# Attention stage of a two-layer image kernel: phases of two slots over seven PSUM banks, waits bank by bank, sums in an idle bank

## The chip, the core and the metric

The kernel runs on one core of a Trainium2 chip. The metric is device time in microseconds (us) of one launch. The engines of the core that matter here are TensorE (PE in the profile, with its weight loads as PEld), ScalarE (ACT), VectorE (DVE), GpSimd (POOL) and the DMA queue of SyncE (SP). Each engine takes its instructions in the order written and waits on semaphores for the others. SBUF is the large on-chip memory; PSUM is the small one that TensorE writes, eight banks of 128 partitions by 512 float32.

## The reference

Two layers run on `x` of shape (2, 256, 64, 64), so two images of 256 channels and 4096 positions. Layer 0 is a state-space block and isn't touched. Layer 1 is attention with eight heads of 32 channels, without an output projection:

```python
x = x + _L0_conv_ref(_gn(x), ...)
x = x + _L1_conv_ref(_gn(x), L1_conv_qkv_w, L1_conv_qkv_b, 8)

# _L1_conv_ref: n = 4096, head_dim = 32
qkv = jnp.einsum('bchw,oc->bohw', x, qkv_w) + qkv_b[None, :, None, None]
qkv = qkv.reshape(b, 3, num_heads, head_dim, n)
q, k, v = (qkv[:, 0], qkv[:, 1], qkv[:, 2])
attn_logits = jnp.einsum('bhci,bhcj->bhij', q, k) * scale
attn_weights = jax.nn.softmax(attn_logits, axis=-1)
out = jnp.einsum('bhij,bhcj->bhci', attn_weights, v)
```

`_gn` normalises groups of eight channels.

## The kernel before, in words

`mamba_stage` (layer 0) takes the first 2010 us or so and also prepares queries, keys and values of image 0. Then `attention` (line 969) works through image 0, prepares image 1 (`prepare`, line 1076) and works through image 1. It is written under a manual schedule: the order in the source is the order on every engine.

**Tiles and slots.** An image has two groups of four heads, and a group has 8 tiles of T = 512 queries, so 16 tiles per image, 32 in all. A tile goes over the 4096 keys in NC = 32 chunks of 128; one tile with one chunk is a *slot* (1024 slots in all), and `c` is the chunk's number. In a slot TensorE makes four matmuls of logits, one per head, keys on the partitions (`logits`, line 1151; matmul at L1162). ScalarE takes their exponentials from PSUM to SBUF (`exponentials`, L1175). TensorE then multiplies values by exponentials into `po`, four column groups of 32 at once (`values`, L1199).

**Row sums.** The denominators are sums of the exponentials over all 4096 keys. Over the partitions they are added by a matmul with `ones` at a tile's end; over the chunks, each head's part is added by another engine:

- Heads 0 and 1 go into `chunk`, a buffer with four places per element (a ring of two). When three new chunks are in it, DVE adds all four places into place 0 of the *other* buffer of the ring (`sum_chunk`, L1184), which the next three chunks fill up. This happens at c = 3, 6, 9, ... 30. At c = 30 the sum goes to `acc_sb` instead, and the exponentials of c = 31 go to a buffer of the ring `e`.
- Heads 2 and 3 go into a ring `e` of five buffers of 128x1024. POOL adds them into `acc_p`: both heads at once for 16 of the chunks (L1230, L1239), and head 3 alone (L1237) for the 15 chunks in `SHARED`, c in {8, 10, 12, 13, 14, 16, 18, 20, 21, 22, 24, 26, 28, 29, 30}. For those, DVE adds head 2 into `acc_2` (L1236; a copy, L1234, for the first). `acc_2` lies in a PSUM bank.

**The end of a tile.** `finish` (line 1241) is a generator that `Slots` resumes once per slot, between other work. It copies `po`, adds the parts (L1249, L1250), lets TensorE sum over the partitions into the PSUM bank of `acc_2` (L1257), copies the sums (L1260), takes reciprocals in four pieces (L1264), multiplies on POOL (L1267), adds bias and the residual (L1270), stores, and keeps two maxima for a range check (L1273, L1274). `end` does this for the last tile of all.

**Phases and PSUM.** Work goes in *phases*. A half slot (two heads) is a unit; a phase has three units, except that each tile ends with two phases of two. The eight banks are three pairs for logits (one tile of two banks per unit), one for `acc_2` and the sums, one for `po`. In step k of `run` (line 1314) ScalarE takes the exponentials of phase k, TensorE does the values of phase k-1 and then the logits of phase k+1. A unit's logits wait until ScalarE has read the pair three units earlier.

**What the code of the page shows as lines.** L1162 logits, L1199 values, L1175 exponentials, L1184 sums of `chunk`, L1236 adds into `acc_2`, L1237 and L1239 adds on POOL, L1250 and L1270 adds in `finish`, L1036 the normalisation of image 1, L463 a step of the group norm of layer 0.

Of the kernel before, what the change touches and what calls it, by code (L numbers as in the profile page):

```python
# [29 lines left out]
def group_norm_scales(nc, small, psum_tile, stats, gmat, eps_t, out):  # L30
# [9 lines left out]
    yield  # L40
    ps = psum_tile()
    for k in range(KC):
        nc.tensor.matmul(ps[:, k : k + 1], lhsT=gmat, rhs=mv[k][:, 0:1], start=True, stop=True)
    for k in range(KC):
        nc.vector.tensor_copy(out[k][:, 0:1], ps[:, k : k + 1])
# [7 lines left out]
    ps = psum_tile()  # L53
    for k in range(KC):
        nc.tensor.matmul(ps[:, k : k + 1], lhsT=gmat, rhs=e[k][:, 1:2], start=True, stop=True)
    yield
    for k in range(KC):
        nc.scalar.activation(e[k][:, 0:1], ps[:, k : k + 1], AF.Ln, bias=eps_t)
        nc.scalar.activation(out[k][:, 1:2], e[k][:, 0:1], AF.Exp, scale=-0.5)


class Slots:
# [10 lines left out]
    def run(self):  # L73
        for entry in list(self.waiting):
            if entry[0] <= self.now:
                try:
                    entry[0] = self.now + (next(entry[1]) or 1)
                except StopIteration:
                    self.waiting.remove(entry)
        self.now += 1  # L80

# [887 lines left out]
def attention(ctx, tc, stats, consts, w, outs, scratch, range_t):  # L969
# [18 lines left out]
    ps_s = ctx.enter_context(tc.tile_pool(name="l1pss", bufs=3, space=PSUM))  # L988
    ps_2 = ctx.enter_context(tc.tile_pool(name="l1ps2", bufs=1, space=PSUM))
# [10 lines left out]
    ep = ctx.enter_context(tc.tile_pool(name="l1e", bufs=5))  # L1000
# [8 lines left out]
    def s_tile():  # L1009
        return ps_s.tile([P, 2, T], F32, name="s", tag="s")  # L1010
# [11 lines left out]
    def load_x(t):  # L1022
        if t >= NT:
            return
        if t < 2:

            if t == 0:
                xn["q"] = p2.tile([P, 4, T], F32R, name="q").bitcast(F32)
            xn[t] = xn["q"][:, KC * t : KC * t + KC, :]
        else:  # L1030
            xn[t] = ep.tile([P, KC, T], F32, name="e")
# [8 lines left out]
    def project(t, i):  # L1040


        pm = s_tile()
        for m in range(KC):
            for c in range(KC):
                nc.tensor.matmul(  # L1046
# [5 lines left out]
                )  # L1052
        halves = chunk().rearrange("p q h t k -> p q (h t k)").rearrange("p q (m t) -> p q m t", t=T)
        for m in range(KC):
            bias = b_qkv[:, i * KC + m : i * KC + m + 1]
            nc.scalar.activation(halves[:, 0, m, :].bitcast(F32R), pm[:, m, :], AF.Identity, bias=bias)
            nc.vector.scalar_tensor_tensor(
                halves[:, 1, m, :].bitcast(F32R), pm[:, m, :], bias, halves[:, 0, m, :], ALU.add, ALU.subtract
            )
            nc.sync.dma_start(scratch.qk[KG + m, i, t].rearrange("s c h t -> (c h) s t"), halves[:, :, m, :])  # L1060

    def project_values(t):
        pm = s_tile()
        flat = pm.rearrange("p a t -> p (a t)")
        for j in range(T // P):
            for c in range(KC):
                nc.tensor.matmul(
# [6 lines left out]
        nc.scalar.copy(v[:, bass.ts(t, T // P), :].rearrange("p s c -> p (s c)"), flat)  # L1074
# [24 lines left out]
    def image(b):  # L1099
# [44 lines left out]
        sizes = [3] * ((2 * NC - 4) // 3) + [2, 2]  # L1144
        bounds = [0, *itertools.accumulate(sizes * (KG * NT))]
        PHASES = [range(*ends) for ends in zip(bounds, bounds[1:])]
        SHARED = [c for c in range(8, NC) if c % 8 in (0, 2, 4, 5, 6)]
        todo = {}
        tiles = {}

        def logits(s, half):
            if s >= S:
                return
            i, c = divmod(s, NC)
            kt, kj = divmod(c * P, T)
            if half == 0:
                todo[s] = Slot()
                todo[s].s, todo[s].e = [], []
            ps = s_tile()
            for j in range(2):  # L1160
                h = 2 * half + j
                nc.tensor.matmul(  # L1162
                    ps[:, j, :], lhsT=keys[i // NT, kt][:, h, kj : kj + P], rhs=queries[i][:, h, :], start=True, stop=True
                )
            todo[s].s.append(ps)

        def exponentials(s, half):
            if half == 0 and s % NC < NC - 1:
                k = place(s % NC)
                first = s % NC == 0 or k == 1 and s % NC > 1  # L1170
                todo[s].chunk = (todo.pop("chunk", None) or chunk()) if first else todo[s - 1].chunk
                e = todo[s].chunk[:, k // 2, :, :, k % 2]
            else:
                e = ep.tile([P, 2, T], F32, name="e")
            nc.scalar.activation(e, todo[s].s[half], AF.Exp, scale=SCALE)  # L1175
            todo[s].e.append(e)
# [9 lines left out]
        def values(first, end):  # L1186

            u = first
            while u < end:
                s, half = divmod(u, 2)  # L1190
                i, c = divmod(s, NC)
                g = i // NT
                width = 2 if half == 0 and u + 1 < end else 1
                cols = slice(half * T // 2, (half + width) * T // 2)
                u += width
                if c == 0 and half == 0:
                    tiles[i].po = ps_o.tile([P, T], F32, name="po")
                for h in range(4):
                    nc.tensor.matmul(  # L1199
                        tiles[i].po[h * D : (h + 1) * D, cols],  # L1200
                        lhsT=v[:, c, g * P + h * D : g * P + (h + 1) * D],
                        rhs=todo[s].e[h // 2][:, h % 2, cols],
# [7 lines left out]
        def add_up(s):  # L1210
            i, c = divmod(s, NC)
            tile_ = tiles[i]
            eb = todo[s].e[1]
            if last(i) and c == NC - 1:
                return
            if last(i) and c == NC - 2:
                pass
            elif c == NC - 2:
                tile_.acc = p1.tile([P, 3, T], F32, name="acc_sb")
                sum_chunk(s, tile_.acc[:, 0:2].rearrange("p h t -> p (h t)"))  # L1220
            elif place(c) == 3:
                todo["chunk"] = chunk()
                sum_chunk(s, todo["chunk"].rearrange("p q h t k -> p q (h t) k")[:, 0, :, 0])
# [7 lines left out]
            elif c in SHARED:  # L1231
                if c == SHARED[0]:
                    tile_.acc_2 = ps_2.tile([P, T], F32, name="acc_2", tag="a2")
# [7 lines left out]
        def finish(i):  # L1241
# [4 lines left out]
            po = p1.tile([P, T], F32, name="po_sb")  # L1246
            nc.vector.tensor_copy(po, d.po)
            acc = d.acc
            nc.vector.tensor_add(acc[:, 2, :], d.acc_2, d.acc_p[:, 0, :])  # L1249
            nc.vector.tensor_add(acc[:, 0:2, :], acc[:, 0:2, :], todo[i * NC + NC - 1].e[0])  # L1250
            res = p3.tile([P, T], F32, name="res")
            nc.sync.dma_start(res, x[g * P : (g + 1) * P, cols])
            yield 3
            ps = ps_2.tile([P, T], F32, name="sums_ps", tag="a2")
            for h in range(4):
                part = acc[:, h, :] if h < 3 else d.acc_p[:, 1, :]
                nc.tensor.matmul(ps[h * D : (h + 1) * D, :], lhsT=ones, rhs=part, start=True, stop=True)  # L1257
            yield
            sums = p1.tile([P, T], F32, name="sums")
            nc.vector.tensor_copy(sums, ps)  # L1260
            yield
            r = p1.tile([P, T], F32, name="r")
# [9 lines left out]
            at = b * KG * NT + i  # L1272
            nc.vector.tensor_reduce(range_t[:, 0, at : at + 1], sums, AX.X, ALU.max)  # L1273
            nc.vector.tensor_reduce(range_t[:, 1, at : at + 1], r, AX.X, ALU.max)  # L1274

        def end():
# [6 lines left out]
            ps = s_tile()[:, 0, :]  # L1283
            acc = p1.tile([P, T], F32, name="acc_end")
            nc.vector.tensor_copy(acc, d.acc_2)
            nc.scalar.activation(res, res, AF.Identity, bias=b_qkv[:, 2 * KC + g : 2 * KC + g + 1])
            terms = [[todo[S - 2].chunk[:, k // 2, h, :, k % 2] for k in range(4)] for h in range(2)]
            terms += [[d.acc_p[:, 0, :], acc], [d.acc_p[:, 1, :]]]

            def sum_up(rounds):  # L1290
                for n in rounds:
                    for h in range(4):
                        n_ = n - 4 + len(terms[h])
                        if 0 <= n_:
                            part = terms[h][n_] if n_ < len(terms[h]) else todo[S - 1].e[h // 2][:, h % 2, :]
                            nc.tensor.matmul(
                                ps[h * D : (h + 1) * D, :], lhsT=ones, rhs=part, start=(n_ == 0), stop=(n == 4)
                            )

            sum_up(range(4))  # L1300
            yield
            sum_up([4])
            r = p1.tile([P, T], F32, name="r")
            for j in range(T // P):
                nc.vector.reciprocal(r[:, bass.ts(j, P)], ps[:, bass.ts(j, P)])
# [5 lines left out]
            nc.vector.tensor_reduce(range_t[:, 0, at : at + 1], ps, AX.X, ALU.max)  # L1311
            nc.vector.tensor_reduce(range_t[:, 1, at : at + 1], r, AX.X, ALU.max)

        def run():
            k = 0
            while k <= len(PHASES) or b == 1 and side.waiting:
                for p in PHASES[k] if k < len(PHASES) else ():
                    s, half = divmod(p, 2)
                    i, c = divmod(s, NC)
                    if half == 0:  # L1320
                        if c == 0:
                            tiles[i] = Slot()
                            load_queries(i + 1)
                        if i % NT == NT - 1 and i < KG * NT - 1 and c % (T // P) == 0:

                            load_keys(i // NT + 1, c * P // T)
                        if b == 1 and 1 <= i <= KG:
                            nc.sync.dma_start(scratch.v[b * KG + i - 1, :, c, :], v[:, c, (i - 1) * P : i * P])
                        if b == 0 and s == S - 24:
                            load_x(0)  # L1330
                            load_x(1)
                        if b == 0 and s == S - 14:
                            normalise(0)
                    if k > 0 or b == 0:
# [225 lines left out]
```

## Time and profile before

| what | us |
|---|---|
| three runs, median (lowest, highest) | 4288.56 (4288.10, 4290.58) |
| the profiled execution: its time, its span | 4289.86, 4288.1 |
| layer 0, with the lead into attention | 0 to 2010 |
| image 0, 16 tiles | 2010 to 3085 |
| preparing image 1 | 3085 to 3180 |
| image 1, 16 tiles | 3180 to 4288 |

The share of busy time over the whole span (PE 96%, DVE 90%, ACT 87%, POOL 87%) is a mean of two unlike layers. In image 0 alone, a stretch of 1075 us, PE is busy 1069.7 us, ACT 1005.8, DVE 964.3 and POOL 940.7, so all four are within 13% of each other. The granted TensorE clock is 1.00 of full speed there, and the DMA engines are busy 16% of the time.

A row of a group reads: line, engine, operation, output <- inputs, shapes, count, then the sum of busy time in us, the mean of one in ns, and the idle time of the engine just before with what ended it. In a timeline the first number is the start, the second the duration, both in us; a number in brackets is the time that the engine stood idle before. Instructions of one engine can overlap at their ends, so the time from one start to the next is shorter than the duration.

### The profile page before, as it was taken

The numbers are of one execution on the slowest core, as the hardware profiler recorded it, in microseconds if no ns is written. First come the engines' busy times: TensorE is split into PE (matmuls) and PEld (weight loads), VectorE is DVE, ScalarE is ACT, GpSimd is POOL, SyncE is SP. The second block draws the span as 40 slices with busy tenths as digits, with TensorE's granted clock in tenths as the row PEclk, the third lists the DMA queues.
The fourth block names the chain that finished last, engine by engine and source line by source line (L and its number), as shares of the span: only waits on it lengthen the run. The fifth ranks groups of instructions, "written<-read, shape, count | busy, mean of one in ns | idle before, by whom it ended". The sixth has DMA issues, their size and how long they took to land.

```text
span 4288.1 us, 58982 instructions
## 1 busy us (share of the span) xinstructions
PE 4119.0 (96%) x21176; PEld 1802.7 (42%) x21176; DVE 3855.6 (90%) x3304; ACT 3729.2 (87%) x4983; POOL 3751.9 (87%) x1913
## 2 busy tenths in 40 slices
PE   6799999999999999988999999999999999999998
PEld 2233333333333343333444444444454444444443
DVE  6899999999999999994988989899849889898998
ACT  5789898999788888874999999999859999999997
POOL 3999999999899999994888988889728989888897
PEclk8899999999999999999999999999999999999999
DMA  6334333344444444447101040110181110401100
GB/s 212 105 114 130 113 113 126 129 133 133 150 144 163 154 141 142 142 167 168 34 24 28 18 106 18 28 30 21 40 262 46 40 28 18 106 18 28 30 21 9
DMA packets 172302, 389.58 MB, mean 91 GB/s; under 512 B 23392, under 2 KB 49760, under 8 KB 163808
## 3 DMA queue, kind: packets, MB, share of 16 engines
q1 hardware_dynamic: 171120, 383.37, 29.4%
q8 instruction: 168, 2.75, 0.3%
q10 hardware_dynamic: 880, 2.36, 0.3%
q14 instruction: 134, 1.10, 0.1%
HBM read 292.33 MB, written 93.32 MB: 90 GB/s over the span
## 4 chain that ended last, share of the span: by engine, by line
PE 82%; DVE 10%; ACT 3%; issue 2%; DMA 1%; POOL 1%; SPq 0%; DVEq 0%; POOLq 0%; ACTq 0%
PE s L1162 25%; PE po L1199 24%; PE mm L448 16%; DVE h L869 6%; PE y L901 4%; PE mm L688 4%; PE bn L448 2%; PE mm L647 2%; DVE bn L860 1%; PE s L1046 1%; PE y L899 1%; PE mm L684 1%; PE sums_ps L1257 1%; ACT da L853 1%; ACT L248 1%
## 5 line engine op out<-in xcount | busy, mean ns | idle before, releaser
L1184 DVE TENSOR_REDUCE chunk<-chunk 128x1024 f32<-128x4096 f32 x288 | 1269.9, 4409 | 169.5 <-ACT chunk L1175 168.2
L1239 POOL TENSOR_TENSOR acc_p<-acc_p,e 128x1024 f32<-128x1024 f32 x479 | 1165.1, 2432 | 121.2 <-ACT e L1175 96.6
L875 POOL TENSOR_TENSOR h<-h,c 128x1024 f32<-128x1024 f32 x512 | 1204.5, 2378 | 33.1 <-issue 15.7
L1162 PE MATMUL s<-q,k 128*128 128x512 f32 x4096 | 1155.0, 415 | 7.3 <-ACT chunk L1175 3.1
L1175 ACT ACTIVATE e<-s 128x1024 f32<-128x1024 f32 x1056 | 1081.8, 1028 | 91.4 <-PE s L1162 58.9
L1175 ACT ACTIVATE chunk<-s 128x1024 f32<-128x1024 f32 x992 | 1117.3, 1126 | 49.3 <-PE s L1162 22.5
L1199 PE MATMUL po<-chunk,v 128*32 128x512 f32 (+1 forms) x5248 | 1057.0, 521 | 0.0
L1199 PE MATMUL po<-e,v 128*32 128x512 f32 (+1 forms) x5504 | 1020.5, 500 | 4.2 <-ACT e L1175 4.2
L1162 PEld LDWEIGHTS s<-q,k 128*128 128x128 f32 x4096 | 713.9, 188 | 624.7 <-ACT e L1175 233.9
L853 ACT ACTIVATE da<-dt_rep,neg_a 128x512 f32<-128x512 f32 x1024 | 695.6, 702 | 107.9 <-DVE h L869 103.7
L1237 POOL TENSOR_TENSOR acc_p<-acc_p,e 128x512 f32<-128x512 f32 x480 | 622.3, 1297 | 95.5 <-ACT e L1175 65.7
L869 DVE TENSOR_TENSOR_SCAN h<-da,state,dbu 128x512 f32<-128x512 f32 x512 | 650.1, 1272 | 14.6 <-PE y L901 7.4
L869 DVE TENSOR_TENSOR_SCAN h<-da,state,bn 128x512 f32<-128x512 f32 x512 | 645.6, 1261 | 11.1 <-PE y L901 5.0
L864 POOL TENSOR_TENSOR dbu<-dtu_rep,b 128x1024 f32<-128x1024 f32 x176 | 418.0, 2375 | 18.8 <-issue 9.1
L448 PE MATMUL bn<-proj,pick 112*128 112x512 f32 x512 | 341.9, 669 | 89.1 <-DVE h L869 86.2
L248 ACT ACT_TABLE_LOAD x312 | 400.3, 1283 | 6.2 <-PEq L1550 0.7
L1199 PEld LDWEIGHTS po<-e,v 128*32 128x32 f32 x5504 | 251.6, 109 | 272.1 <-issue 105.3
L860 DVE TENSOR_TENSOR bn<-dtu_rep,bn 128x512 f32<-128x512 f32 x512 | 345.4, 677 | 18.0 <-PE bn L448 8.0
L1199 PEld LDWEIGHTS po<-chunk,v 128*32 128x32 f32 x5248 | 240.2, 108 | 251.2 <-issue 251.2
L1236 DVE TENSOR_TENSOR acc<-acc,e 128x512 f32<-128x512 f32 x448 | 309.5, 691 | 17.4 <-DVE acc L1236 0.5
L901 PE MATMUL y<-h,sum 128*32 128x512 f32 x2048 | 299.3, 613 | 6.9 <-POOL h L875 6.8
L448 PE MATMUL mm<-yn,w_in 128*128 128x512 f32 x512 | 255.2, 623 | 7.9 <-ACT yn L538 3.8
(163 smaller groups left out, 4182.9 us busy)
## 6 DMA issues: line engine op xcount, KB each, us to landing
dt_rep<-dt_dram SPq DMA_DIRECT2D x128, 512.0 KB, 5.0
dtu_rep<-dtu_dram SPq DMA_DIRECT2D x128, 512.0 KB, 5.3
k<-qk_dram SPq DMA_DIRECT2D x62, 512.0 KB, 7.6
q<-qk_dram SPq DMA_DIRECT2D x124, 256.0 KB, 4.8
b<-bc_dram SPq DMA_DIRECT2D x64, 256.0 KB, 3.1
c<-bc_dram SPq DMA_DIRECT2D x64, 256.0 KB, 3.8
dt_dram<-dt SPq DMA_DIRECT2D x64, 256.0 KB, 2.3
dtu_dram<-lw SPq DMA_DIRECT2D x64, 256.0 KB, 3.6
```

Source lines behind the costliest of these rows:

```text
L248: self.nc.scalar.preload_act_table_set(self.TABLES[task.table])
L448: nc.tensor.matmul(out, lhsT=lhsT, rhs=rhs, start=(i == 0), stop=(i == len(pairs) - 1))
L853: nc.scalar.activation(da[j].tile, dt.tile[:, j, :], AF.Exp, scale=scale)
L869: nc.vector.tensor_tensor_scan(h.tile[:, j, :], da[j].tile, dbu, initial, ALU.mult, ALU.add)
L875: nc.gpsimd.tensor_tensor(h.tile, h.tile, rows_c.tile.unsqueeze(1).to_broadcast([P, 2, T]), ALU.mult)
L901: nc.tensor.matmul(y.tile[j * PQ : (j + 1) * PQ, :], lhsT=sum4, rhs=pair[j // 2].h.tile[:, j % 2, :], start=False, stop=(qd == NQ - 1),)
L1162: nc.tensor.matmul(ps[:, j, :], lhsT=keys[i // NT, kt][:, h, kj : kj + P], rhs=queries[i][:, h, :], start=True, stop=True)
L1175: nc.scalar.activation(e, todo[s].s[half], AF.Exp, scale=SCALE)
L1184: nc.vector.tensor_reduce(out, terms, AX.XY, ALU.add)
L1199: nc.tensor.matmul(tiles[i].po[h * D : (h + 1) * D, cols], lhsT=v[:, c, g * P + h * D : g * P + (h + 1) * D], rhs=todo[s].e[h // 2][:, h % ...
L1237: nc.gpsimd.tensor_add(acc_p[:, 1, :], acc_p[:, 1, :], eb[:, 1, :])
L1239: nc.gpsimd.tensor_add(acc_p, acc_p, eb)
```

## The change

**Banks and phases.** `s_tile` (three pairs) becomes one tile `banks` of seven banks; `po` keeps the eighth. Waits between engines over it are made bank by bank by a new class `Banks`, which removes the tile's own dependences and adds one for each bank that an instruction touches. A phase is always two slots (eight matmuls of logits, 16 phases per tile). ScalarE takes four instructions per phase as before per two slots, but over 1, 2, 2 and 3 banks; `ORDERS` has the banks of even and odd phases. The bank of the single exponential is written a second time within its phase, after that exponential.

**Buffers.** The ring `e` has three buffers of 128x2048 (a phase each) in place of five of 128x1024 (a slot each). The exponentials of c = 31 go into `chunk` as well, so the sum at c = 30 goes to the other buffer of the ring, as at other chunks, and the next tile's c = 0 takes the buffer that this sum reads.

**Sums.** `acc_2` goes from PSUM to SBUF (`p1`), its first copy too. In `finish`, `acc` is now the sum of two places of `chunk`; `acc_2` is added to `acc_p` a phase later, in place; the matmuls with `ones` follow another phase later and write the bank that is idle in that phase (`spare`); ScalarE, not DVE, copies the sums out. Reciprocals are taken in place, four pieces, a phase each.

**The rest.** The group norm of image 1 uses the spare bank, with copies on ScalarE. `prepare` uses three pairs of banks in turn. The order of the other loads and stores is kept; a phase issues them for two slots.

```diff
+class Banks:
+    def note(self, made, engine, banks, writes):
+        ins = made.ins
+        need = []
+        for b in banks:
+            last = self.written.get(b)
+            if last and last[0] != engine:
+                need.append(last[1])
+            need += [r for e, r in self.read.get(b, {}).items() if e != engine]
...
-    ps_s = ctx.enter_context(tc.tile_pool(name="l1pss", bufs=3, space=PSUM))
-    ps_2 = ctx.enter_context(tc.tile_pool(name="l1ps2", bufs=1, space=PSUM))
+    ps_s = ctx.enter_context(tc.tile_pool(name="l1pss", bufs=1, space=PSUM))
...
-    ep = ctx.enter_context(tc.tile_pool(name="l1e", bufs=5))
+    ep = ctx.enter_context(tc.tile_pool(name="l1e", bufs=3))
...
+    banks = ps_s.tile([P, 7, T], F32, name="s")
+    ORDERS = (
+        (0, (5, 6), (3, 4), (1, 2, 0)),
+        (3, (5, 6), (0, 1), (2, 4, 3)),
+    )
+    def spare():
+        return 1 if side.phase % 2 else 4
...
+        def phase_logits(k):
+            single, first, second, three = ORDERS[k % 2]
+            low = min(three)
+            places = [(0, 2, single)]
+            places += [(0, h, first[h]) for h in range(2)]
+            places += [(1, h, second[h]) for h in range(2)]
+            places += [((0, 3), (1, 2), (1, 3))[bank - low] + (bank,) for bank in three]
+            for n, (late, h, bank) in enumerate(places):
+                if n == 7:
+                    e = phases[k] = ep.tile([P, 4, T], F32, name="e")
+                    exponential(e[:, 0, :], single, 1)
+                mm = nc.tensor.matmul(banks[:, bank, :], ...)
+                log.note(mm, "pe", [bank], True)
...
+        def exponentials(k):
+            for late, pair in enumerate((first, second)):
+                s = 2 * k + late
+                at = place(c)
+                if c == 0 or at == 1 and c > 1:
+                    todo[s].chunk = todo.pop("chunk", None) or chunk()
+                exponential(terms, pair[0], 2)
+                if at == 3 and not (last(s // NC) and c == NC - 2):
+                    todo["chunk"] = chunk()
+                    sum_chunk(s, ...)
+            exponential(e[:, 1:4, :], low, 3)
+            for s in (2 * k, 2 * k + 1):
+                add_up(s)
...
-                    tile_.acc_2 = ps_2.tile([P, T], F32, name="acc_2", tag="a2")
+                    tile_.acc_2 = p1.tile([P, T], F32, name="acc_2")
                     nc.vector.tensor_copy(tile_.acc_2, eb[:, 0, :])
                 else:
                     nc.vector.tensor_add(tile_.acc_2, tile_.acc_2, eb[:, 0, :])
...
         def finish(i):
+            terms = [todo[i * NC + NC - 1].chunk[:, 0, :, :, k] for k in range(2)]
+            acc = p1.tile([P, 2, T], F32, name="acc_sb")
+            nc.vector.tensor_add(acc, terms[0], terms[1])
             nc.vector.tensor_copy(po, d.po)
-            nc.vector.tensor_add(acc[:, 2, :], d.acc_2, d.acc_p[:, 0, :])
-            nc.vector.tensor_add(acc[:, 0:2, :], acc[:, 0:2, :], todo[i * NC + NC - 1].e[0])
-            yield 3
+            yield 2
+            nc.vector.tensor_add(d.acc_p[:, 0, :], d.acc_p[:, 0, :], d.acc_2)
+            yield 2
+            bank = spare()
+                mm = nc.tensor.matmul(banks[h * D : (h + 1) * D, bank, :], lhsT=ones, rhs=part, ...)
-            nc.vector.tensor_copy(sums, ps)
+            log.note(nc.scalar.copy(sums, banks[:, bank, :]), "act", [bank], False)
+            yield 2
+            nc.vector.tensor_reduce(range_t[:, 0, at : at + 1], sums, AX.X, ALU.max)
+            r = sums
             for j in range(T // P):
                 nc.vector.reciprocal(r[:, bass.ts(j, P)], sums[:, bass.ts(j, P)])
                 yield 2
```

## The prediction

> **What bounds the kernel now.** I read the page's shares first, then the stages. Layer 0 ends near 2010 us and no instruction of it changes, so the question is one attention tile. In the page, the chain that ended last is TensorE for 82% of the span, with the two attention lines on top:
>
> ```profile
> PE 82%; DVE 10%; ACT 3%; issue 2%; DMA 1%; POOL 1%; SPq 0%; DVEq 0%; POOLq 0%; ACTq 0%
> ```
>
> Next the busy time of the engines (PE, PEld, DVE, ACT, POOL) in two stretches, each from one end-of-tile add (L1250) to the next:
>
> ```profile
> 2144.73:2212.60 67.87, 67.84 (x473) 31.82 (x474) 61.39 (x37) 63.52 (x65) 59.81 (x32) 1.00 0.10 25
> 2212.60:2280.45 67.85, 67.82 (x473) 31.85 (x474) 61.36 (x37) 63.58 (x65) 59.80 (x32) 1.00 0.10 25
> ```
>
> A tile takes 67.85 us, and TensorE is never idle in it. But DVE is busy for 61.4 of it, POOL for 59.8, ScalarE for 63.5: whoever takes 4 us from TensorE meets the others. The chain of waits within a tile shows what a phase costs:
>
> ```profile
> 2194.56 1.60 PE s L1162 x6
> 2196.16 1.52 PE po L1199 x13
> ...
> 2342.27 1.12 PE s L1162 x4
> 2343.39 1.04 PE po L1199 x6
> ```
>
> Six logits take 1.60 us, four 1.12; values of one and a half slots 1.52, of one slot 1.04. What doesn't shrink with the work is paid per phase. The timeline of DVE over a tile's end, which is where DVE is idle at all:
>
> ```profile
> 2341.48 4.42 DVE L1184 TENSOR_REDUCE acc_sb<-chunk 128x1024 f32<-128x4096 f32 x1 [0.43 <-ACT chunk L1175]
> ...
> 2352.31 4.42 DVE L1184 TENSOR_REDUCE chunk<-chunk 128x1024 f32<-128x4096 f32 x1 [2.79 <-ACT chunk L1175]
> 2356.64 0.68 DVE L1260 COPY sums<-sums_ps 128x512 f32<-128x512 f32 x1
> 2359.43 4.42 DVE L1184 TENSOR_REDUCE chunk<-chunk 128x1024 f32<-128x4096 f32 x1 [2.10 <-ACT chunk L1175]
> ```
>
> After c = 30 DVE has to wait for c = 3 and c = 6; in the rest of the tile it is full. Last, DVE beside POOL, from their timelines:
>
> ```profile
> 2315.56 0.74 DVE L1270 SCALAR_TENSOR_TENSOR res<-po_sb,b_qkv,res 128x512 f32<-128x512 f32 x1
> ...
> 4239.98 2.77 DVE L1270 SCALAR_TENSOR_TENSOR res<-po_sb,b_qkv,res 128x512 f32<-128x512 f32 x1
> ```
>
> ```profile
> 4239.80 2.41 POOL L1239 TENSOR_TENSOR acc_p<-acc_p,e 128x1024 f32<-128x1024 f32 x1
> 4242.29 1.62 POOL L1237 TENSOR_TENSOR acc_p<-acc_p,e 128x512 f32<-128x512 f32 x1
> ```
>
> L1270 has two large inputs in SBUF. Started while POOL was between instructions it takes 0.74 us; started 0.18 us after a POOL add it took 2.77, ending 0.54 after that add ended (4242.21), and the next POOL add took 1.62 in place of 1.29. So the two exclude each other. L1236, with `acc_2` in PSUM, shows none of it: 0.69 us in 187 cases, beside a POOL that is nearly always busy.
>
> **The change, part by part.**
>
> *TensorE.* Logits of two slots: 1.60 + 2 x (1.60 - 1.12)/2 = 2.08. Values: 1.52 + (1.52 - 1.04) = 2.00. A phase is 4.08, a tile 16 x 4.08 + 0.86 (the sums' matmuls, from the chain) = 66.1 against 67.85. (The 0.86 is the chain's row at 2150.03.) TensorE alone would free 1.75 us per tile.
>
> *ScalarE.* Starts are 1.00 apart after a `chunk` instruction and 0.89 after an `e` one (2302.91, 2303.91, 2304.80). One bank plus three cost what two plus two do if time is linear in size, so a phase is 2 x 1.00 + 2 x 0.90 = 3.80, under TensorE's 4.08. The copy of the sums adds about 0.6 per tile (an estimate between half of 0.90 and L853's 0.70 for 128x512). Single about 0.53, three about 1.27.
>
> *A new wait at c = 0.* Before, c = 0 took a buffer whose sum was three slots old. Now it takes the one that the sum of c = 30 reads, so the exponentials of c = 0 wait for that sum; behind them on ScalarE wait the rest of the phase, then TensorE's next logits. From there DVE's tile can be added up as one lap, from the end of the sum at c = 30 to the next:
>
> 1. To the start of the sum at c = 3: four `chunk` instructions (4.00), a three and a single (1.80), handovers about 0.2: 6.0. Under it DVE does add c = 30 (0.70), `acc` (1.22) and the copy of `po` (0.69).
> 2. To the start of the sum at c = 6. `finish` adds `acc_2` to `acc_p` behind the sum of c = 3, TensorE's sums wait for that, ScalarE's copy for these, and behind the copy stand the single and the pair of c = 6: 4.33 + 0.70 + 0.86 + 0.6 + 0.53 + 1.00 + some 0.4 of handovers = 8.4.
> 3. Then DVE is full: nine sums of 4.33 (39.0), 13 adds of 0.70 (9.1), the first copy 0.68, two maxima 1.2, four reciprocals of 0.86 (3.4), L1270's work 0.66: 54.0.
>
> Together 68.4, already 0.55 over 67.85. Nothing is hidden here: DVE becomes the ring that the others wait in.
>
> *`acc_2` in SBUF.* Now 13 adds in the lap, the add into `acc_p` and L1270 have two SBUF inputs beside POOL; with the first copy, 16 instructions. The copy's nearest rows: L1234 into PSUM takes 0.68 beside POOL, L1036 from SBUF to SBUF took up to 1.52 beside it, 0.54 without; I count it as L1036. The Trainium skill ("SBUF — State Buffer", "Who interferes with whom") says that a float32 copy within SBUF may run in a mode that holds the port shared with GpSimd; by that the copy belongs among the 16, and without the rule and L1036 the sum would be 0.75 lower per tile. No run before shows such a copy.
>
> The price of one: no wait (0) up to a whole POOL add (2.41), more if POOL gives no gap. I take the wait that an arrival at a random moment finds. Per tile POOL has 16 instructions of 2.41 and 16 of 1.30; the squares sum to 93 + 27 = 120, half of it over a tile of 80 us is 0.75. It comes off a little, since 0.2 of the instruction runs ahead of its wait (0.54 against 0.74), and goes up, since three pairs of adds stand back to back and the second meets a POOL add just begun. So 16 x 0.75 = 12.0 and a lap of 80.4. POOL loses 0.33 each (1.62 - 1.29), 16 x 0.33 + 59.8 = 65, and has room.
>
> *At nothing.* `Banks` issues no instruction; the ring `e` gives POOL two phases (8 us) for adds of at most 2 x 2.48; loads and stores are the same ones, `q` landing in 4.8 us with a tile's lead; group norm and `prepare` are some instructions once. If POOL fell two phases behind, the single would wait for it.
>
> *Sum.* 31 laps x (80.4 - 67.85) = 389; on the profiled span of 4288.1, 4677. The span is 0.5 us from the median shown, so nothing is corrected.
>
> **The rivals.**
>
> *The ring alone (7%).* Adds find POOL idle; no price for SBUF. For it: L1250, 31 cases, always 1.21 to 1.22. Against: POOL stands idle when L1250 starts, and the POOL add that begins under it takes 2.67 in place of 2.40. Then 31 x 0.55 = 17: 4305.
>
> *TensorE's gain comes through (6%).* The lap is under 66.1, because sums overlap more than I add or the wait at c = 0 is covered; decided from there. Then 31 x 1.75 = 54 less: 4234. For it: TensorE is the chain now, and has 16 phases per tile in place of 22. Against: the lap has 54 us of DVE work behind c = 6, and before, the same rows left DVE 6.5 us idle of 67.85.
>
> *DVE is starved (7%).* In layer 0 a one-element L463 took 6.41 us, over three POOL instructions that overlapped (starts 1085.36, 1087.66, 1089.97). The skill's rule on that page has the loser blocked until the first is done, so one POOL instruction at most, which by itself would leave the 12.0 above; the row shows three. In attention POOL leaves 0.08 between adds (2314.38 + 1.29 to 2315.76), and L1270 got in there. If each waits one whole mean add more (1.86), that is 30 on top per lap: 31 x 42.4 = 1310, so 5600. It decides from a mean wait of 1.2, which no single POOL add explains on average.
>
> **How the numbers follow.** The forecast, both the ring and the exclusion, has 80%: 4677. Its ends: 0.25 per instruction gives a lap of 72.4 and 4430, 1.2 gives 87.6 and 4900. That is also the range; what lies outside is the three rivals, 20%. Faster by over 0.2%: 6%. Within 0.2% (about what a measurement of this kernel can tell from no change): 4%, the lower part of the ring alone. Slower: 90%.
>
> **What would show it.** In the profile after: the tile near 80 us; TensorE idle some 15 us of it, ended by ScalarE; the adds into `acc_2` at 0.69 to 3.1 us, mean near 1.4; POOL adds of 1.6 and 2.7 among them; the first exponentials of a tile waiting for DVE by some 4 us; ScalarE's copy waiting for TensorE. I am wrong on the price if adds stay at 0.69, on the ring if DVE is idle in the second half of a tile, and on all of it if TensorE stays without gaps.

## The result, and the profile after

| kernel | median us (lowest, highest) | runs |
|---|---|---|
| before | 4288.33 (4286.69, 4290.58) | 4 |
| after | 4717.09 (4712.17, 4720.11) | 4 |

The ratio is 1.0998 with a 95% interval of 1.0979 to 1.1017: the changed kernel is 10% slower. Its profiled execution took 4719.62 us, its span is 4717.3, so the profile stands for the runs.

The place is the attention tile. Two tiles of the changed kernel, each from one end-of-tile add (now L1310) to the next, in the view by windows; the columns are the window, its length, the busy time with the count of instructions of PE, PEld, DVE, ACT and POOL, then the granted TensorE clock, the DMA share and GB/s:

```profile
2409.60:2491.65 82.05, 71.53 (x392) 32.45 (x392) 74.45 (x36) 63.36 (x66) 61.57 (x32) 0.94 0.08 20
2491.65:2573.50 81.85, 69.88 (x392) 31.38 (x392) 74.25 (x36) 63.30 (x66) 61.88 (x32) 0.98 0.11 26
```

A tile takes 81.85 us where it took 67.85. 31 x 14.0 = 434, and 428.8 were lost: the whole loss is here. TensorE executes fewer instructions per tile than before and yet stands idle for 10.5 to 12.0 us of it, at a granted clock that was 1.00 and is 0.94 to 0.98. DVE's busy time has gone from 61.4 to 74.4 us, with one instruction less. So it is not more work for DVE; the same work takes longer. The groups of POOL's adds and of the adds into `acc_2` (L1297) on the page after:

```profile
L1300 POOL TENSOR_TENSOR acc_p<-acc_p,e 128x1024 f32<-128x1024 f32 x479 | 1211.7, 2530 | 118.6 <-ACT e L1226 86.5
...
L1298 POOL TENSOR_TENSOR acc_p<-acc_p,e 128x512 f32<-128x512 f32 x479 | 648.0, 1353 | 403.8 <-ACT e L1226 383.3
...
L1297 DVE TENSOR_TENSOR acc<-acc,e 128x512 f32<-128x512 f32 x447 | 598.4, 1339 | 20.2
```

The adds into `acc_2` have a mean of 1339 ns against 690 before. Their spread says more than the mean: from 0.67 to 2.90 us, half of them under 0.92. An add that takes 0.67 as a rule and 2.90 at worst is waiting for something. For what, the timelines of DVE and POOL over the same moments show; a row with x2 is two instructions in one stretch:

```profile
2419.42 2.75 DVE L1315 TENSOR_TENSOR acc_p<-acc_p,acc 128x512 f32<-128x512 f32 x1
...
2451.13 4.57 DVE L1297 TENSOR_TENSOR acc<-acc,e 128x512 f32<-128x512 f32 x2
2455.62 2.88 DVE L1337 SCALAR_TENSOR_TENSOR res<-po_sb,b_qkv,res 128x512 f32<-128x512 f32 x1
```

```profile
2416.75 4.88 POOL L1300 TENSOR_TENSOR acc_p<-acc_p,e 128x1024 f32<-128x1024 f32 x2 [1.72 <-ACT e L1226]
...
2450.92 2.39 POOL L1300 TENSOR_TENSOR acc_p<-acc_p,e 128x1024 f32<-128x1024 f32 x1
2453.85 1.30 POOL L1298 TENSOR_TENSOR acc_p<-acc_p,e 128x512 f32<-128x512 f32 x1 [0.54 <-ACT e L1226]
2455.23 2.73 POOL L1300 TENSOR_TENSOR acc_p<-acc_p,e 128x1024 f32<-128x1024 f32 x1
```

Read the ends. POOL's pair ends at 2421.63, L1315 at 2422.17, 0.54 later. POOL's add of 2453.85 ends at 2455.15, the second of the two L1297 at 2455.70, 0.55 later. POOL's next add ends at 2457.96 and L1337 at 2458.50, 0.54 later. Each time DVE ends one fixed step behind the POOL add that it met. The same step was seen once before the change, in L1270 beside POOL.

The other part of the result is the start of a tile. ScalarE's timeline and then DVE's, with the idle time in brackets:

```profile
2409.18 2.06 ACT L1226 ACTIVATE chunk<-s 128x1024 f32<-128x1024 f32 x2 [3.62 <-DVE chunk L1259]
...
2423.33 0.59 ACT L1325 COPY sums<-s 128x512 f32<-128x512 f32 x1 [0.72 <-PE s L1320]
```

```profile
2404.67 4.41 DVE L1259 TENSOR_REDUCE chunk<-chunk 128x1024 f32<-128x4096 f32 x1
...
2409.60 1.22 DVE L1310 TENSOR_TENSOR acc_sb<-chunk 128x1024 f32<-128x1024 f32 x1
2410.73 0.68 DVE L1311 COPY po_sb<-po 128x512 f32<-128x512 f32 x1
2415.09 4.42 DVE L1259 TENSOR_REDUCE chunk<-chunk 128x1024 f32<-128x4096 f32 x1 [3.67 <-ACT chunk L1226]
...
2425.44 4.42 DVE L1259 TENSOR_REDUCE chunk<-chunk 128x1024 f32<-128x4096 f32 x1 [3.27 <-ACT chunk L1226]
...
2431.36 4.36 DVE L1259 TENSOR_REDUCE chunk<-chunk 128x1024 f32<-128x4096 f32 x1
...
2486.73 4.41 DVE L1259 TENSOR_REDUCE chunk<-chunk 128x1024 f32<-128x4096 f32 x1
```

The first and the last row are the sums of c = 30 of this tile's start and end. At c = 0 ScalarE waits 3.62 us for the first, as the prediction's third part says. Then DVE waits 3.67 for ScalarE before c = 3 and 3.27 before c = 6: the two wait for each other in turn, so what is added to either lengthens the tile. From 2425 on DVE is full to the tile's end.

### The profile page after: what moved, and what is told of

It is laid out like the page before. It is cut to its first block, busy times and chain, and to the rows that moved or that the text cites. A ratio compares the mean times of both kernels' runs of the same rounds, so it can differ in the third digit from the quotient of the medians.

```text
span 4717.3 us, 52851 instructions
## 1 busy us (share of the span) xinstructions
PE 4220.6 (89%) x18620; PEld 1808.8 (38%) x18620; DVE 4263.5 (90%) x3269; ACT 3722.7 (79%) x5016; POOL 3816.1 (81%) x1912
## 3 DMA queue, kind: packets, MB, share of 16 engines
q10 hardware_dynamic: 880, 2.36, 0.2%
## 5 line engine op out<-in xcount | busy, mean ns | idle before, releaser
L1259 DVE TENSOR_REDUCE chunk<-chunk 128x1024 f32<-128x4096 f32 x319 | 1402.2, 4395 | 237.1 <-ACT chunk L1226 236.0
L1215 PE MATMUL s<-q,k 128*128 128x512 f32 x4096 | 1209.8, 436 | 327.9 <-ACT chunk L1226 283.7
L1300 POOL TENSOR_TENSOR acc_p<-acc_p,e 128x1024 f32<-128x1024 f32 x479 | 1211.7, 2530 | 118.6 <-ACT e L1226 86.5
L1215 PEld LDWEIGHTS s<-q,k 128*128 128x128 f32 x4096 | 764.3, 201 | 1018.8 <-ACT chunk L1226 680.0
L1226 ACT ACTIVATE e<-s 128x512 f32<-128x512 f32 (+1 forms) x1024 | 1038.5, 1035 | 105.6 <-PE s L1215 41.8
L1268 PE MATMUL po<-chunk,v 128*32 128x512 f32 x4096 | 1072.0, 644 | 0.0
L1268 PE MATMUL po<-e,v 128*32 128x512 f32 x4096 | 990.3, 605 | 0.0
L1297 DVE TENSOR_TENSOR acc<-acc,e 128x512 f32<-128x512 f32 x447 | 598.4, 1339 | 20.2
L1268 PEld LDWEIGHTS po<-e,v 128*32 128x32 f32 x4096 | 195.2, 110 | 301.9 <-issue 301.9
L1268 PEld LDWEIGHTS po<-chunk,v 128*32 128x32 f32 x4096 | 191.6, 109 | 208.0 <-issue 207.7
```

Of the source, the lines that this page charges most:

```text
L1215: mm = nc.tensor.matmul(banks[:, bank, :], lhsT=keys[i // NT, kt][:, h, kj : kj + P], rhs=queries[i][:, h, :], start=True, stop=True,)
L1226: done = nc.scalar.activation(e, ps, AF.Exp, scale=SCALE)
L1259: nc.vector.tensor_reduce(out, terms, AX.XY, ALU.add)
L1268: nc.tensor.matmul(tiles[i].po[h * D : (h + 1) * D, :], lhsT=v[:, c, g * P + h * D : g * P + (h + 1) * D], rhs=todo[s].e[h], start=(c == 0 ...
L1297: nc.vector.tensor_add(tile_.acc_2, tile_.acc_2, eb[:, 0, :])
L1300: nc.gpsimd.tensor_add(acc_p, acc_p, eb)
```

## The experiments

The theory is that of the prediction: a ring of ScalarE and DVE that costs half a microsecond per tile by itself, and on top a wait of every two-input DVE instruction for the POOL instruction that it meets. The rivals left standing by the result were that the ring, the new phases or the bank-by-bank waits made most of the loss, and that DVE was only an onlooker.

| run | edit | us | per lap against its base |
|---|---|---|---|
| e1_before_sbuf | kernel before, `acc_2` in SBUF | 4643.83 | +11.4 |
| e2_one_input | after, adds into `acc_2` with one input | 4407.58 | -10.0 |
| e3_no_port | e2, the two other adds with one input | 4338.41 | -2.2 |
| e5_no_port_no_wait | e3, c = 0 doesn't wait for DVE | 4325.16 | -0.4 |
| e4_no_wait | after, c = 0 doesn't wait for DVE | 4631.08 | -2.8 |
| w1_no_pairs | another plan of the sums | 4456.29 | 1.0383 of before |
| w2_flat | w1, buffer laid out flat | 4245.63 | 0.9893 of before |
| w3_flat_ones | w2, the sum added by TensorE | 4258.31 | 0.9923 of before |

The first five are single runs; the kernel before took 4291.91 beside e1, e2, e3 and e5, and 4290.63 (median of 7) beside e4. The fourth column is the difference to the base (before, after, e2, e3 and after) divided by 31 laps; for the last three runs it is the ratio to the kernel before. The kernel after stood beside a kernel before of 4288.33, so a difference between it and e2 or e4 is uncertain by 2 to 4 us.

**One line alone, on the kernel before.**

```diff
-                    tile_.acc_2 = ps_2.tile([P, T], F32, name="acc_2", tag="a2")
+                    tile_.acc_2 = p1.tile([P, T], F32, name="acc_2")
...
-            acc = p1.tile([P, T], F32, name="acc_end")
-            nc.vector.tensor_copy(acc, d.acc_2)
+            acc = d.acc_2
```

> The kernel before with one part of the change alone: acc_2 in SBUF, all else as it was (three pairs of banks, 22 phases per tile). Theory (DVE adds with two SBUF inputs and POOL exclude each other): 16 instructions per tile wait 0.75 us on average, the mean of the adds into acc_2 goes from 0.69 to 1.2-1.5 us, a tile takes 73.4 (61.4 busy + 12.0) to 78 us, so 4460 to 4615 us. Rival (the time is lost by the new phases, banks and the wait at c = 0, and not by where acc_2 lies): adds stay at 0.69, 4288 us within 0.5%.

Measured 4643.83, so 352 us lost by the place of one tile of 128x512, with the old phases, the old rings and no new wait. That is a miss, 29 us above the theory's band, and far from the rival's 4288. The groups of DVE in image 0 by this kernel (its lines are those of before):

```profile
L1236 DVE TENSOR_TENSOR acc<-acc,e 128x512 f32<-128x512 f32 x159 | 207.6, 1306 | 5.8
...
L1270 DVE SCALAR_TENSOR_TENSOR res<-po_sb,b_qkv,res 128x512 f32<-128x512 f32 x12 | 28.6, 2381 | 0.0
L1234 DVE COPY acc<-e 128x512 f32<-128x512 f32 x12 | 23.0, 1914 | 0.0
L1250 DVE TENSOR_TENSOR acc_sb<-acc_sb,e 128x1024 f32<-128x1024 f32 x11 | 22.2, 2017 | 0.0
```

The adds went from 690 to 1306 ns here (1340 over both images), as in the changed kernel. L1270, whose operands this edit doesn't touch, went from 740 to 2381, which suggests that it now comes at another moment of POOL's work. The end-of-tile adds wait too: over both images L1250 went from 1215 to 1713, and L1249, which now reads `acc_2` in SBUF, from 681 to 1094. With 14 x 0.65 = 9.1, the copy's 1.2 (675 to 1845 over both images), L1270's 1.6 (2330 over both images), L1249's 0.4 and L1250's 0.5, DVE has 12.8 us more per tile; 11.4 per lap were lost.

So the 6.5 us which DVE had idle in each tile before were hardly a reserve: the mean over this kernel's tiles is still 5.2 (single tiles have from 1.7 to 8.4), and only 1.3 of the 12.8 went into them. The theory's band had counted on 1.9 to all of the 6.5. They are waits for ScalarE, which waits for DVE's sums and for TensorE, and TensorE in its turn waits for DVE's copy of `po` (46.3 us in nine waits, from 2200 to 2900). Two tiles of this kernel, with 6.9 and 1.7 us of idle DVE:

```profile
2085.08:2163.37 78.29, 73.96 (x490) 33.65 (x483) 71.42 (x37) 63.44 (x64) 59.59 (x32) 0.94 0.08 21
2163.37:2241.55 78.18, 67.50 (x459) 30.67 (x461) 76.49 (x37) 63.47 (x64) 64.63 (x33) 0.97 0.08 21
```

**The adds with one input, in the kernel after.**

```diff
-                    nc.vector.tensor_add(tile_.acc_2, tile_.acc_2, eb[:, 0, :])
+                    nc.vector.tensor_reduce(tile_.acc_2[:, 0:1], eb[:, 0, :], AX.X, ALU.max)
```

> The changed kernel with the 14 adds into acc_2 of a tile as maxima over the same 512 elements: one SBUF input, 0.68 us, same place and same order. It leaves out most of head 2's part of the row sums. Theory: the 9.1 us of waits per tile (14 x (1.34 - 0.69)) go, tile 72.8 us, 4435 us; the end-of-tile add into acc_p (2.5 us) and the add of the residual (2.8 us) still wait for POOL. Rival (the DVE ring at the tile's start sets the time and the waits fill what would be idle): 4717 us within 1%.

Measured 4407.58, 309.5 us less than the kernel after, 27 less than expected and far from the rival's 4717. A maximum over 512 elements takes as long as an add that meets nobody, and reads the same new exponentials beside the same POOL. In image 0, by groups:

```profile
L1297 DVE TENSOR_REDUCE acc<-e 128x1 f32<-128x512 f32 x178 | 120.1, 675 | 7.8
...
L1315 DVE TENSOR_TENSOR acc_p<-acc_p,acc 128x512 f32<-128x512 f32 x12 | 30.6, 2548 | 0.0
L1337 DVE SCALAR_TENSOR_TENSOR res<-po_sb,b_qkv,res 128x512 f32<-128x512 f32 x13 | 28.7, 2209 | 0.0
```

675 ns beside POOL's adds, while the two that kept two inputs stayed above 2 us. 14 x (1.339 - 0.675) = 9.3 per tile, 10.0 measured.

The maximum lacks two things, the second input and the 512 elements written to SBUF. That it isn't the writing is shown by the sums of `chunk` in the kernel after, which have one input and write 1024 elements to SBUF beside the same POOL (by source line: count, then lowest, median and highest ns):

```profile
L1259 DVE TENSOR_REDUCE chunk<-chunk x319: 4351/4406/4422, 2005.8 to 4691.6; 128x1024 f32<-128x4096 f32 x160
```

None of the 319 was lengthened.

**The two others with one input as well.**

```diff
-            nc.vector.tensor_add(d.acc_p[:, 0, :], d.acc_p[:, 0, :], d.acc_2)
+            nc.vector.tensor_reduce(d.acc_p[:, 0, 0:1], d.acc_p[:, 0, 1:T], AX.X, ALU.max)
...
-            nc.vector.scalar_tensor_tensor(res, po, bias, res, ALU.add, ALU.add)
+            nc.vector.tensor_reduce(res[:, 0:1], po, AX.X, ALU.max)
```

> As e2_one_input, and the add into acc_p and the add of bias and residual are maxima over one SBUF input too; only the first copy of acc_2 and the add of two places of chunk are left with the port. It leaves out head 2's sums, and bias and residual of all tiles but the last. Theory: what is left is the ring of the prediction, 68.4 us per tile and 0.6 for the copy, so 4305 to 4325 us. Rival (the exclusion is only half of the loss): over 4400 us. Rival (TensorE's gain comes through once the port is free): 4234 us.

Measured 4338.41, 13 us above the upper end, and near neither rival (over 4400, and 4234). The tile takes 69.2 to 69.9 us. What the theory had too small is the wait of the copy L1295, which in this kernel meets POOL at a worse moment: 0.6 was allowed for it, and in image 0 its mean is 1.73, which is 1.05 over 0.68; 31 x 0.45 = 14 us. The rows of one tile, DVE's timeline, from the sum of c = 30 to the next:

```profile
2284.11 4.41 DVE L1259 TENSOR_REDUCE chunk<-chunk 128x1024 f32<-128x4096 f32 x1
...
2294.57 4.42 DVE L1259 TENSOR_REDUCE chunk<-chunk 128x1024 f32<-128x4096 f32 x1 [3.42 <-ACT chunk L1226]
2298.90 0.68 DVE L1315 TENSOR_REDUCE acc_p<-acc_p 128x1 f32<-128x511 f32 x1
2302.85 4.42 DVE L1259 TENSOR_REDUCE chunk<-chunk 128x1024 f32<-128x4096 f32 x1 [3.28 <-ACT chunk L1226]
...
2313.05 1.92 DVE L1295 COPY acc<-e 128x512 f32<-128x512 f32 x1
...
2353.34 4.41 DVE L1259 TENSOR_REDUCE chunk<-chunk 128x1024 f32<-128x4096 f32 x1
```

With only the copy and the add of L1310 left to meet POOL, the ring can be read off: 8.28 us from the sum of c = 3 to that of c = 6. The copy costs 1.92 - 0.68 = 1.24 more than where it meets nobody (0.67 at the least in e1, also into SBUF).

**c = 0 without its wait for DVE.** The sum of c = 30 reads `v` in place of the buffer that c = 0 takes; e5 is e3 with this edit, e4 the kernel after with it.

```diff
-                    sum_chunk(s, todo["chunk"].rearrange("p q h t k -> p q (h t) k")[:, 0, :, 0])
+                    sum_chunk(s, todo["chunk"].rearrange("p q h t k -> p q (h t) k")[:, 0, :, 0], c == NC - 2)
...
+            if other:
+                terms = v.rearrange("p c d -> p (c d)")[:, 0 : 8 * T].rearrange("p (m q k) -> p m q k", q=2, k=2)
```

> As e3_no_port, and the sum at c = 30 reads the values in place of the chunk buffer, with the same shape, so the exponentials of c = 0 no longer wait for it. It leaves out also the sums of heads 0 and 1 over all chunks but the last two. Theory (with neither exclusion nor the wait at c = 0, TensorE's 16 phases set the time): 66.1 us per tile or a little less, 4200 to 4240 us. Rival (the wait at c = 0 costs nothing by itself): the same as e3_no_port within 0.3%.

> The changed kernel with one edit: the sum at c = 30 reads the values in place of the chunk buffer, so the exponentials of c = 0 do not wait for it; the DVE adds with two SBUF inputs stay. It leaves out the sums of heads 0 and 1 over all chunks but the last two. Theory (waits of DVE on POOL and the ring add up): DVE's 75 us per tile with its waits stay and only idle time of DVE at the tile's start shrinks, 75 to 80 us per tile, 4510 to 4660 us. Rival (the wait at c = 0 is what makes the exclusion dear): within 1% of e5_no_port_no_wait, 4325 us.

e5 measured 4325.16, a miss: 13 us were won where about 100 to 140 were expected, and TensorE's 66.1 us per tile didn't come through (69.04). The gain is 0.31%, where the rival had at most 0.3%. The waits of e3 and of e5 over the same 700 us (who waited for whom: total us, times, longest):

```profile
ACT chunk L1226 <- DVE chunk L1259: 30.2, 20, 2.4
```

```profile
ACT chunk L1226 <- PE po L1270: 21.2, 10, 2.1
...
ACT chunk L1226 <- DVE chunk L1261: 7.0, 9, 0.9
```

The wait for DVE is nearly gone, and at the same place, once per tile, ScalarE now waits 2.1 us for TensorE. The buffer that c = 0 takes holds the exponentials of c = 28 to 30, and TensorE's values still read them. So two readers hold this buffer; the one that came last hid the other. Taking one away shows the other. In w1 and w2 below c = 0 takes an older buffer, and in the 600 us looked at of each ScalarE waits at this place for neither.

e4 measured 4631.08, within its band and far from its rival's 4325. The same edit was worth 2.8 us per lap with the exclusion in place, and 0.4 without it.

**A plan with one two-input add of DVE per tile.** In w1 the seven banks and the phases of two slots stay. Head 2 of the even chunks is exponentiated straight into a buffer of three places, which DVE adds up with an instruction of one input. The sums of c = 30 and 31 go to tiles of their own, so c = 0 takes a buffer that is three slots old. ScalarE and POOL do the work of L1337. TensorE adds the sum of `even` in a second round of matmuls with `ones`. Of DVE's adds with two SBUF inputs, the one at the tile's end stays.

```diff
+                todo["even"] = e2.tile([P, T, 3], F32, name="even")
+                nc.vector.tensor_reduce(todo["even"][:, :, 0], even, AX.X, ALU.add)
...
+                if c == NC - 1:
+                    terms = todo[s].late = p1.tile([P, 2, T], F32, name="late")
...
+                if c == NC - 2 and not last(s // NC):
+                    tiles[s // NC].acc = p1.tile([P, 2, T], F32, name="acc_sb")
+                    sum_chunk(s, tiles[s // NC].acc.rearrange("p h t -> p (h t)"))
...
+            nc.scalar.activation(res, res, AF.Identity, bias=b_qkv[:, 2 * KC + g : 2 * KC + g + 1])
             nc.gpsimd.tensor_mul(po, po, r)
-            nc.vector.scalar_tensor_tensor(res, po, bias, res, ALU.add, ALU.add)
+            nc.gpsimd.tensor_add(res, po, res)
```

> A version that keeps the seven banks and phases of two slots and takes both costs away: the exponentials of head 2 of even chunks go straight into a buffer of three places, which DVE sums by one-input reductions every second phase (7 of 128x512 from 128x1536 per tile, some 1.7 us each), no DVE add with two SBUF inputs is left beside POOL but the end-of-tile add of 1.22; c = 30 is summed into its own buffer and c = 31 goes to another, so c = 0 takes a buffer three slots old; the residual is added by POOL after a bias on ScalarE; the extra buffer for keys goes and keys are loaded four slots later. Theory: TensorE's 16 phases of 4.08 and sums of 1.2 to 1.6 set the time, 66.5 to 67 us per tile, 4235 to 4270 us. Rival (one of DVE, POOL, ScalarE, each at 61 to 64 us of work per tile, binds): 4270 to 4340 us.

Measured 4456.29, 1.0383 of before (1.0366 to 1.0400): a miss, though TensorE was busy for all of the 600 us looked at. Its tile took 73.02 us and a phase's values 2.36 in place of 2.00. TensorE's groups in image 0:

```profile
L1282 PE MATMUL po<-e,v 128*32 128x512 f32 x789 | 317.0, 598 | 0.0
...
L1282 PE MATMUL po<-chunk,v 128*32 128x512 f32 x1014 | 259.3, 629 | 0.0
L1282 PE MATMUL po<-even,v 128*32 128x512 f32 x262 | 204.2, 865 | 0.0
```

The same matmul, the same output. `e` is read element by element, `chunk` with a step of 8 bytes, `even` with a step of 12, and that one takes 865 ns. 16 x 0.36 = 5.8 us of the 6.7 that the tile is above 66.3.

**The same, flat.** w2 lays the three places one after another, and POOL adds the finished sum to `acc_p` in place of the second round of matmuls with `ones`.

```diff
-                        todo["even"] = e2.tile([P, T, 3], F32, name="even")
+                        todo["even"] = e2.tile([P, 3, T], F32, name="even")
...
+                    nc.gpsimd.tensor_add(acc_p[:, 0, :], acc_p[:, 0, :], todo[s].even[:, 0, :])
```

> w1_no_pairs with the three places of the new buffer one after the other (each 512 elements in a row) and not side by side, so TensorE reads head 2 of even chunks without a step of 12 bytes; and the sum of the even chunks is added by POOL before the matmuls with ones, not by a second round of these. Theory (in w1_no_pairs the step alone makes a values phase 2.36 us in place of 2.00): values back at 2.00, phase 4.07, sums 1.2, 66.3 us per tile, 4225 to 4260 us. Rival (the step isn't it, but the third buffer or the column group's other partner): phases stay at 4.42, 4450 us. Rival (DVE now pays for reading three places 2 KB apart): its reductions go from 1.73 to over 2.5 us and DVE binds, 4280 to 4350 us.

Measured 4245.63 (4241.06 to 4247.09), inside its band and 0.9893 of before (0.9877 to 0.9910): 45 us faster than before, 471 faster than after. TensorE's group and a tile's window:

```profile
L1282 PE MATMUL po<-even,v 128*32 128x512 f32 x290 | 151.7, 605 | 0.0
```

```profile
2341.60:2407.90 66.30, 66.30 (x396) 30.75 (x392) 63.48 (x26) 63.83 (x67) 62.88 (x37) 1.00 0.10 25
```

The tile is 66.30 us and TensorE is busy for all of it at clock 1.00. DVE is busy for 63.5 of it, more than in the kernel before, and costs nothing: in the 600 us from 2300 no engine waits for it. The exclusion isn't gone, for the end-of-tile add that is left takes 1.74 us in the mean, against 1.23 in w1.

**Who adds the sum.** w3 is w2 with the second round of matmuls with `ones` on `even` again, in place of POOL's add. So it differs from w1 in the layout alone.

```diff
-                    nc.gpsimd.tensor_add(acc_p[:, 0, :], acc_p[:, 0, :], todo[s].even[:, 0, :])
...
+            for n, parts in enumerate(([acc[:, 0, :], acc[:, 1, :], d.acc_p[:, 0, :], d.acc_p[:, 1, :]], [None, None, even, None])):
```

> w2_flat, with the sum of the even chunks taken in a second round of the matmuls with ones (0.43 us more of TensorE per tile, 1.4 us less of POOL). Theory (TensorE binds, POOL has room): w2_flat plus 0.4 us per tile, 12 us. Rival (POOL's last adds of a tile hold up the sums): faster than w2_flat.

Measured 4258.31, 0.9923 of before (0.9907 to 0.9940), 12.7 us above w2, with a tile of 66.72, as the theory had it. Here TensorE bounds the tile, and its 0.41 us more per tile comes out in full. Against w1 it is 198 us faster, and the layout is the only difference: the step was the cause there.

## Why the prediction was right

4677 was predicted and 4717 measured, inside the range. The 40 us between them are two errors: the exclusion cost 1.6 us per lap more than the sum had, and the ring 0.4 less (31 x 1.2 = 37). The lap can be checked in the tile of the timelines above, from the end of the sum of c = 30 (2404.67 + 4.41 = 2409.08) to the next (2486.73 + 4.41 = 2491.14):

| step | predicted | after | e3 |
|---|---|---|---|
| 1, to the sum of c = 3 | 6.0 | 6.0 | 6.05 |
| 2, from there to the sum of c = 6 | 8.4 + 0.75 | 10.35 | 8.28 |
| 3, DVE full | 54.0 + 15 x 0.75 | 65.7 | 54.9 |
| lap | 80.4 | 82.06 | 69.2 |

- **The ring (68.4).** Right, within 0.4 us at each step. e3's first step is from the end of its sum of c = 30 (2288.52) to 2294.57, its third from 2302.85 to the next such end (2357.75). Take the copy's 1.24 off its third step and 53.7 stand against 54.0, and 68.0 against 68.4 for the lap. That the wait at c = 0 exists is shown by ScalarE's 3.62 us. Not named in the prediction: the second reader of that buffer, TensorE, behind DVE. It cost nothing here, being hidden, but it voided the expectation for e5.
- **The price of exclusion (16 x 0.75).** The mechanism was right, shown by e1 and e2 from both sides; the size was 12.0 per tile and measured 13.6: the adds 14 x 0.65 = 9.1, L1315 1.8 (2.51 against 0.69), L1337 2.1 (2.82 against 0.74), the copy 0.6 (1.32 against 0.68). The picture behind the 0.75, an arrival at a random moment, holds for none of them: the work repeats from tile to tile, and nearly every wait repeats with it. In 29 tiles of the kernel after the second of the 14 adds took 0.67 us, the third 1.60 or 1.61, the fourth 2.71 to 2.75 and the last 0.68; only two of the 14 varied widely, from 0.98 to 2.90 and from 0.67 to 1.77. So the adds' mean excess of 0.65 is an average over fixed places, and that it came near 0.75 is in part luck, though e1, with the adds at other moments, has the same 0.65. For a single instruction the average says little. L1315 at 2419.42 comes just behind the start of a POOL add, the second of a pair that began at 2416.75, and L1337 at 2455.62 behind that of 2455.23; their medians are 2.53 and 2.89. L1315 stands alone in step 2, on the way to TensorE's sums and ScalarE's copy: in this tile it cost 2.06 in place of 0.75, and the step is 1.2 over its 9.15. That is the term that was mis-sized, most of the 1.66 that the lap is long; step 3 is 0.45 over, though L1337 cost 2.14 there, because other waits in it were under 0.75.
- **A row of the prediction.** L1270 at 2315.56 did not start between two POOL instructions, as the prediction says: it started 0.11 us before the POOL add of 2314.38 ended (2315.67). It took 0.74 all the same, which fits the prediction's 0.2 us that run ahead of the wait.
- **The copy among the 16.** It takes 1.32 us beside POOL (1.84 in e1, 1.73 in e3's image 0), 0.68 when it went into PSUM. The Trainium skill ("SBUF — State Buffer", "Who interferes with whom") says that a copy can run in a mode that contends with GpSimd for the shared ports; all three rows agree.
- **Starved DVE.** Not seen: no add into `acc_2` took more than 2.90 us, one POOL add and the fixed step, and the mean wait of the adds was 0.65.
- **POOL has room.** Right. Its adds take 2.73 where they meet one of DVE and 2.39 where not, and POOL is busy for 61.6 us of 82.05, under the 65 of the sum.
- **TensorE's 66.1 per tile.** Right to 0.2, though it shows only in w2 (66.30), where nothing else binds. In the kernel after, TensorE's idle time of 10.5 to 12.0 is under the 15 of the prediction, because the same matmuls were busy for 71.5 and 69.9 us, at a granted clock of 0.94 and 0.98. The clock alone, as an estimate, makes 70.3 and 67.4 of 66.1; the rest isn't explained by a run here.
- **ScalarE's copy waiting for TensorE.** Seen, 0.72 us in the tile shown.

The rival of the ring alone is nearly the one that e3 built, and it lost 47 us beside the runs of its chip rather than 17, mostly for the copy that stayed in it (31 x 1.0 = 31). The rival that TensorE's gain comes through was right about the gain and wrong about this kernel: w2, with other sums, is at 4245.63, 12 us above its 4234.

## What to carry to other kernels

Count the SBUF inputs of each DVE instruction that runs beside a busy GpSimd, and count a copy within SBUF as well: it has one input and took 1.32 us in place of 0.68. Here an accumulator in PSUM made an add cost 0.69 us and one in SBUF 1.34, and moving that one accumulator cost 352 us of 4290; a bank freed that way has to bring more than this. Where a DVE sum has to leave PSUM, a reduction over places side by side has one input and didn't wait here; but look at the step with which TensorE reads them. And when a buffer's next writer waits, ask for all of its readers, not for the one that the profile names. Where a schedule repeats, look at the moment at which a single instruction meets the other engine; an average wait says little about it.

## What the runs showed of the hardware

- **A step of 12 bytes slows TensorE and ScalarE.** Matmuls with float32 operands of 128x512 took 598 to 607 ns on consecutive elements, 629 to 640 at a step of 8 bytes and 865 at 12; ScalarE's exponential of 128x512 took 605 ns into consecutive elements and 877 at a step of 12. The Trainium skill ("SBUF — State Buffer", "Door 1: The DMA port swizzle (why `[64,N]` ≈ `[32,N]`)") says that SBUF has lines of 16 bytes and that full speed needs two accesses to each. By that, as an estimate, a step of 8 gives two and a step of 12 gives 4/3 on average, and the rows fit it. The same passage gives 4 float32 as the distance that one can stride for free; the 865 and 877 ns, at a step of 3 float32, don't agree with that. For DVE the flat layout is the dearer one: its reduction over three places took 1735 ns with the places side by side, and 1916 ns with the places 2 KB apart.
- **The granted clock was lower where TensorE had more and longer gaps.** Over 600 to 900 us of image 0 it was 1.00 with TensorE never idle (before, w1, w2, w3) or idle for 2.9% (e5), 0.99 at 3.2% (e3) and 5.1% (e2), 0.96 at 10.1% (e1) and 11.3% (e4), and 0.95 at 13.3% (after). Single tiles don't keep this order: the two of e1 above, with 5.5% and 13.7%, had 0.94 and 0.97. TensorE's longest wait was 4.3 to 6.6 us in the three kernels at 0.95 and 0.96, and at most 1.9 us in e2, e3 and e5. No run tells the share of idle time from the length of the gaps.
